# Layer 0's selective scan: delta turned by TensorE into PSUM instead of a transposed copy in memory

## The chip, the cores and the metric

The kernel runs on one core of one Trainium2 chip. The metric is the device time of one execution in microseconds (us), as the median of several runs of the whole program, four layers one after the other.

## The reference, cut to what matters

Layer 0 is a two-dimensional selective scan over 4 images of 64 x 64 tokens. Only the scan matters here:

```python
delta = jax.nn.softplus(delta + delta_bias[None, :, None])
def step(h, inp):
    u_i, d_i, b_i, c_i = inp
    dA = jnp.exp(d_i[..., None] * A)
    h = h * dA + (d_i * u_i)[..., None] * b_i[:, None, :]
    y = jnp.einsum('gdn,gn->gd', h, c_i)
    return (h, y)
```

There are 256 channels d with 16 states n each. Every image is scanned four times, with u read by rows, by columns, and both backwards, while delta, B and C are the same sequence in all four. The results are summed, normalised and projected. Layers 1 to 3 follow and are the same before and after the change.

## The kernel before, in words

**Chunks and passes.** A sequence of 4096 tokens is cut into 64 chunks of 64. The 256 channels are two halves h of 128. One step I of the loop treats one chunk of one half of one image, in all four directions; there are 4 x 2 x 64 = 512 steps. Sixty-four steps of one image and one half are called a pass. Direction is counted by j (0 forward, 1 backward) and kp (rows, columns). `quads` are groups of four chunks, whose deltas (`dp`, loaded by `load`, L564) and decays (`dA`, `decay`, L587) are kept together.

**One step** (L788 to L842). Its engines' work, in the order in which it is written out:

- `fetch(I + 2)` (L596) issues on SP the loads of the chunk two steps ahead: C broadcast (`ct`), u with tokens on the partitions (`xo`: 64 forward tokens, then 64 backward), delta with tokens on the partitions (`dt`: 64 tokens forward, then the same 64 backwards), and diagonals of B (`dg`).
- `diagonal(I + 1)` (L631) makes those diagonals on ACT in the passes of h = 0 and stores them for h = 1.
- `products(I, kp)` (L657): TensorE multiplies `du` (delta times u) with the diagonals of B, 16 small matmuls for each kp, into two tiles `db` of PSUM, one for each j. Each fp32 matmul appears as two records in the trace, so one call is 32 records. Three `db` tiles of two banks each exist in turn.
- `scan` (L678): DVE adds the carry to the first column of `db` (L684) and runs the scan (L687), once for each j. POOL then forms the carry for the next chunk (L694) and multiplies the states with C (L702).
- `total(I - 2, part)` (L709): TensorE sums the states over n into the PSUM tile `yp` (L722), in two parts of 16 records; after the second part ACT copies the four directions out (L736).
- `inputs(I + 1)` (L641): DVE forms `du` of the next step, `xo` times `dt` (L644).

So the order on TensorE is: products for kp 0, total's first part, side work, products for kp 1, side work, total's second part. On DVE: two scans, `inputs` of the next step, two scans. TensorE, ACT and DVE keep this written order (a manual schedule).

**Side work.** The generator `beside` is advanced by one piece (to its next `yield`) twice in a step, and a third time in every fourth step of h = 0. In passes of h = 0 it carries `back` of the previous image (normalisation and projection) and `front` of the next one; in passes of h = 1 it carries `middle` of the next image: the convolution (L376), transposes (L394), projections (L406, L424, L436) and the softplus that gives delta. What is left is run out at once shortly before the end of h = 1. For the first image, `front` and `middle` run ahead of the loop, outside the manual schedule.

**Where the transposed delta comes from.** At the end of each block of 512 tokens `middle` has delta, channels on the partitions, in `rs`. It stores it (`dl`). It then turns each half with four transposes (L465), copies the result out on ACT (L475), multiplies it with the matrix `flip` to reverse the tokens within each chunk (L470), and copies that out too. Both are stored to `dT` (L477), and `fetch` reads `dt` from there. That takes four pieces of `beside` per block, of 14.

**PSUM** [...]six in the three `db` tiles, one for `yp` (half used), and one (`bg`) for the side work.

Of the kernel before, what the change touches and what calls it, by code (L numbers as in the profile page):

```python
# [14 lines left out]
P = 128  # L15
B = 4
HW = 64
S = HW * HW
NT = S // P
D = 128  # L20
BLK = 512
# [6 lines left out]
TC = 64  # L28
NCHUNK = S // TC
NH0 = NST // 2  # L30
QC = 4
# [28 lines left out]
def tl(pool, shape, tag, dtype=F32, bufs=None):  # L60
    return pool.tile(shape, dtype, name=tag, tag=tag, bufs=bufs)
# [99 lines left out]
def layer0(cm, x, W, x1, also, kept):  # L161


    tc, nc = cm.tc, cm.nc
    wl = kept.enter_context(tc.tile_pool(name="l0k", bufs=1))
    dr = kept.enter_context(tc.tile_pool(name="l0dram", bufs=2, space=DRAM))
    with ExitStack() as ctx:
        ctx.enter_context(nc.allow_non_contiguous_dma(reason="parameters laid over partitions"))
        wp = ctx.enter_context(tc.tile_pool(name="l0w", bufs=1))
        big = ctx.enter_context(tc.tile_pool(name="l0big", bufs=3))  # L170
        tmp = ctx.enter_context(tc.tile_pool(name="l0t", bufs=10))
        t4 = ctx.enter_context(tc.tile_pool(name="l0t4", bufs=4))
        yb = ctx.enter_context(tc.tile_pool(name="l0y", bufs=2))
        p2 = ctx.enter_context(tc.tile_pool(name="l0p2", bufs=2))
        db = ctx.enter_context(tc.tile_pool(name="l0db", bufs=3, space=PSUM))
        pp = ctx.enter_context(tc.tile_pool(name="l0pp", bufs=1, space=PSUM))
# [30 lines left out]
            part = cm.ident[rows, rows]  # L207
            nc.vector.tensor_copy(mask[rows, :], part[:, ::-1] if r > 1 else part)

        flip = tl(wp, [P, P], "flip")  # L210
        nc.vector.memset(flip, 0.0)
        for p in range(2):
            half = slice(p * TC, (p + 1) * TC)
            nc.vector.tensor_copy(flip[half, half], cm.ident[half, half][:, ::-1])

        both = tl(wp, [P, TC], "both")
        nc.vector.tensor_copy(both[0:TC, :], cm.ident[0:TC, 0:TC])
        nc.vector.tensor_copy(both[TC:P, :], cm.ident[TC:P, TC:P])
# [17 lines left out]
        dA = []  # L236
        for i in range(2):
            t = tl(wp, [P, QC, 2, NH0, TC], f"dA{i}")
# [2 lines left out]
            dA.append(t)  # L241


        yp = tl(pp, [P, 2, 2, TC], "yp")

        BT = tl(wp, [P, NCHUNK, NST], "BT")

# [3 lines left out]
        for i in range(2):  # L251
            t = tl(wp, [P, 8, PADW], f"padded{i}")
# [9 lines left out]
        img = {}  # L262

        def begin(b):
            img[b] = {
                "zs": tl(dr, [P, 2, S], "zs"),
                "dl": tl(dr, [2, P, S], "dl_d"),
                "ct": tl(dr, [NCHUNK, NST, TC], "ct_d"),
                "xT": tl(dr, [2, S, P], "xT_d"),
                "dT": tl(dr, [2, NCHUNK, 2, TC, P], "dT_d"),  # L270
                "y0": tl(dr, [P, 2, S], "y0_d"),
                "yr": tl(dr, [P, 2, S], "yr_d"),
            }
# [91 lines left out]
        def middle(b, bank, pool, tag, ahead):  # L365

            ready = [shifted(i, pool, tag) for i in range(ahead)]
            for k in range(NBLK):
                cols = slice(k * BLK, (k + 1) * BLK)
                xa = []  # L370
                for h in range(2):
                    ps = bank()
                    x3 = ready.pop(0)
                    for dx in range(3):
                        for g in range(4):
                            nc.tensor.matmul(  # L376
                                ps[g * CG : (g + 1) * CG, :], lhsT=cdiag[:, 4 * h + g, dx, :],
                                rhs=x3[g // 2][:, g % 2, :].rearrange(
                                    "p (r w) -> p r w", w=PADW
                                )[:, :, dx : dx + HW],  # L380
                                start=(dx == 0), stop=(dx == 2),
# [10 lines left out]
                    ps = bank()  # L392
# [4 lines left out]
                    t = tl(tmp, [P, 4, P], "t2k")  # L397
# [5 lines left out]
                ps = bank()  # L403
# [16 lines left out]
                ps = bank()  # L420
                pb = ps[:, 0 : 8 * NST].rearrange("p (c n) -> p c n", n=NST)
                for c in range(8):
                    for j in range(2):
                        nc.tensor.matmul(  # L424
                            pb[j * TC : (j + 1) * TC, c, :],
                            lhsT=xr[0:n, c, :] if j else xd[0:n, c * TC : (c + 1) * TC],
                            rhs=cm.ident[0:n, RANK : RANK + NST], start=True, stop=True,
                        )
                nc.vector.tensor_copy(BT[:, 8 * k : 8 * k + 8, :], pb)
                rs = []  # L430
# [24 lines left out]
                    nc.sync.dma_start(img[b]["dl"][h, :, cols], r)  # L455
                    rs.append(r)

                yield
                for h in range(2):
                    t = None  # L460
                    for j in range(2):
                        ps = bank()
                        if j == 0:
                            for i in range(4):
                                nc.tensor.transpose(  # L465
                                    ps[:, i * P : (i + 1) * P], rs[h][:, i * P : (i + 1) * P],
                                    cm.ident,
                                )
                        else:
                            nc.tensor.matmul(  # L470
                                ps, lhsT=flip, rhs=t.rearrange("p t c -> p (t c)"),
                                start=True, stop=True,
                            )
                        t = tl(tmp, [P, 4, P], "t2k")
                        nc.scalar.copy(t, ps.rearrange("p (t c) -> p t c", c=P))  # L475
                        for i in range(2):
                            nc.sync.dma_start(  # L477
                                img[b]["dT"][h, 8 * k + i : 8 * k + 8 : 2, j]
                                .rearrange("t r c -> r t c"), t[i * TC : (i + 1) * TC],
                            )  # L480
                        yield

        def back(b, bank, tmp=tmp, t4=t4):

# [79 lines left out]
        def load(q):  # L564

            b, h, c = place(q * QC)
            cols = slice(c * TC, (c + QC) * TC)
            dp = tl(p2, [P, 2, QC, TC], "dp")
            for p in range(2):
                nc.sync.dma_start(  # L570
                    dp[p * TC : (p + 1) * TC].rearrange("p g c t -> p g (c t)"),
                    img[b]["dl"][h, :, cols].rearrange("(g d) t -> d g t", d=TC),
                )
            return {"dp": dp, "dA": dA[q % 2], "h": h}

        def begun(w):

# [18 lines left out]
        def fetch(I):  # L596

            b, h, c = place(I)
            ct = tl(p2, [P, NH0, TC], "ct", bufs=4)
            for p in range(2):  # L600
                nc.sync.dma_start(
                    ct[p * TC : (p + 1) * TC].rearrange("p n t -> p (n t)"),
                    img[b]["ct"][c, p * NH0 : (p + 1) * NH0, :].rearrange("n t -> (n t)")
                    .unsqueeze(0).to_broadcast([TC, NH0 * TC]),
                )
            xo = tl(p2, [P, 2, P], "xo", bufs=3)
            dt = tl(p2, [P, P], "dt", bufs=3)
            nc.sync.dma_start(dt, img[b]["dT"][h, c].rearrange("j r c -> (j r) c"))
            xT = img[b]["xT"][h]
            rows = (  # L610
                slice(c * TC, (c + 1) * TC), slice(c, S, TC),
                slice(S - (c + 1) * TC, S - c * TC), slice(TC - 1 - c, S, TC),
            )
            for j in range(2):
                for kp in range(2):
                    nc.sync.dma_start(
                        xo[j * TC : (j + 1) * TC, kp, :], xT[rows[2 * j + kp], :]
                    )
            dg = tl(p2, [P, NST, QR], "dg", bufs=3)
            if h:  # L620
                nc.sync.dma_start(dg, dg_d[c].rearrange("p (n t) -> p n t", t=QR))
            inp[I] = {"ct": ct, "xo": xo, "dg": dg, "dt": dt}

        def first(w):
            nc.scalar.activation(w["a0"], w["a0"], AF.Exp)
# [5 lines left out]
        def diagonal(q):  # L631

            if q["h"]:
                return
            for n in range(NST):
                nc.scalar.activation(  # L636
                    q["dg"][:, n, :], mask, AF.Copy, scale=BT[:, q["c"], n : n + 1]
                )
            nc.sync.dma_start(dg_d[q["c"]], q["dg"].rearrange("p n t -> p (n t)"))

        def inputs(q):  # L641

            q["du"] = tl(p2, [P, 2, P], "du")
            nc.vector.tensor_tensor(  # L644
                q["du"], q["xo"], q["dt"].unsqueeze(1).to_broadcast([P, 2, P]), ALU.mult
            )

        def after(later, earlier):
            tc.add_manual_dep(
                later.ins, earlier.ins.name,  # L650
                mybir.DependencyInfo(
                    mybir.DependencyClass.Sync, mybir.DependencyReason.DATA
                ),
                reason="row groups of one bank",
            )

        def products(q, kp):  # L657
            bs = [tl(db, [P, 2 * NH0, TC], "db") for _ in range(2)]
            mm = None
            for half in range(2):  # L660
                if half:
                    nc.tensor.drain()
                for i in range(8):
                    j, r, p = i // 4, i // 2 % 2, i % 2
                    g = r ^ half
                    rows = slice((2 * j + r) * QR, (2 * j + r + 1) * QR)
                    t0 = (r ^ j) * QR
                    nc.tensor.matmul(  # L668
                        bs[j][
                            p * TC : (p + 1) * TC, g * NH0 : (g + 1) * NH0, t0 : t0 + QR  # L670
                        ],
                        lhsT=q["du"][rows, kp, g * TC : (g + 1) * TC],
                        rhs=q["dg"][rows, p * NH0 : (p + 1) * NH0, :],
                        start=True, stop=True,
                    )
            return bs
# [97 lines left out]
        fetch(1)  # L774
        nxt = start(0)
        diagonal(nxt)
        inputs(nxt)
        beside, clock = None, [0]

# [7 lines left out]
        with tc.manual_schedule(engines=engines):  # L787
            for I in range(N):  # L788
# [27 lines left out]
                if I + 1 < N:  # L816
                    nxt = start(I + 1)
                    diagonal(nxt)
                bs = products(now, 0)
                scan(I, now, 0, bs, st, carry, new)  # L820
                if I > 1:
# [1535 lines left out]
```

## Time and profile before

| | |
|---|---|
| median of 3 runs | 10872.56 us (10855.62 to 10873.84) |
| profiled execution | 10860.27 us |
| its span | 10858.5 us |
| TensorE (PE) busy | 8928.9 us, 82% |
| VectorE (DVE) busy | 7823.8 us, 72% |
| ScalarE (ACT) busy | 5313.2 us, 49% |
| GpSimd (POOL) busy | 5452.4 us, 50% |
| before the loop of layer 0 | 0 to 341 us |
| the loop of 512 steps | 341 to about 6245 us |
| layers 1 to 3 | the rest |

A row of the profile reads: line, engine, operation, written tile <- read tiles with shapes, number of instructions | busy time in us, mean of one in ns | idle time of the engine just before them, and what ended most of it. PEld is TensorE's loading of weights, which overlaps its matmuls. The granted clock is the share of full speed that TensorE's throttle allowed. A row of the timeline gives the start and the duration in us, and in brackets the engine's idle time before it. Ends of matmuls are modelled, and spans on POOL are rough.

### The profile page before, as it was taken

Reading aid. Unit: us, or ns where it says so; the run is one execution under the profiler, and the core shown is the slowest. Engines: PE = TensorE matmul, PEld = TensorE weight load, DVE = VectorE, ACT = ScalarE, POOL = GpSimd, SP = SyncE. Lnnn points to the kernel's source line nnn. Section 1 sums busy time; section 2 is a strip of 40 time slices with the busy share of each in tenths; the row PEclk is TensorE's granted clock in tenths of the full one; section 3 lists DMA queues with packets and bytes.
Section 4 is the critical chain, followed back from the end, with each engine's and each line's share of the span. In section 5 each row is a group of like instructions: output and inputs, shape, how many; then the busy total and the mean of one; then the engine's idle time right before and its main releaser. Section 6 shows DMA issues by size and latency. Waiting matters only on the chain. (4 is left out here: it accounts for less than half of the span.)

```text
span 10858.5 us, 190052 instructions
## 1 busy us (share of the span) xinstructions
PE 8928.9 (82%) x72040; PEld 4226.5 (39%) x72040; DVE 7823.8 (72%) x10667; ACT 5313.2 (49%) x13151; POOL 5452.4 (50%) x2661
## 2 busy tenths in 40 slices
PE   6668998779887788887788846999999956998886
PEld 2333443334333333333333323444444434544442
DVE  1799999999999999999999965546361132445546
ACT  5557554556444565445532124767676613333321
POOL 0579999879888888888899920000000000000000
PEclk7789998889888889888888968999999976577767
DMA  5434554335443345443333231111100083012101
GB/s 150 105 91 128 145 140 110 103 98 153 131 119 110 109 117 141 130 119 102 99 94 94 74 117 38 36 35 36 32 27 16 16 226 70 26 37 57 41 20 47
DMA packets 1155618, 960.91 MB, mean 88 GB/s; under 512 B 191940, under 2 KB 905384, under 8 KB 1148312
## 3 DMA queue, kind: packets, MB, share of 16 engines
q1 hardware_dynamic: 1140888, 898.41, 29.2%
q0 software_dynamic: 13824, 50.34, 2.6%
q8 instruction: 579, 9.49, 0.4%
q14 instruction: 327, 2.68, 0.1%
HBM read 616.68 MB, written 331.61 MB: 87 GB/s over the span
## 5 line engine op out<-in xcount | busy, mean ns | idle before, releaser
L687 DVE TENSOR_TENSOR_SCAN big<-dA,db 128x1024 f32<-128x1024 f32 x2048 | 4679.5, 2286 | 81.9 <-PE db L668 3.1
L702 POOL TENSOR_TENSOR big<-big,ct 128x2048 f32<-128x2048 f32 x1024 | 4648.2, 4539 | 78.7 <-DVE big L687 0.2
L668 PE MATMUL db<-dg,du 32*64 32x256 f32 x32768 | 1952.0, 427 | 822.1 <-DVE db L684 674.5
L722 PE MATMUL yp<-big,both 128*64 128x256 f32 x16384 | 2368.9, 438 | 66.2 <-ACT yc L736 58.2
L722 PEld LDWEIGHTS yp<-big,both 128*64 128x64 f32 x16384 | 1250.6, 155 | 1152.0 <-issue 752.8
L668 PEld LDWEIGHTS db<-dg,du 32*64 32x64 f32 x32768 | 672.3, 138 | 2079.6 <-issue 1909.5
L736 ACT COPY yr<-yp 128x64 f32<-128x64 f32 x1024 | 224.4, 220 | 1618.2 <-PE yp L722 1617.8
L1480 PE MATMUL av<-e,x 128*128 128x512 f32 x2048 | 974.0, 592 | 4.6 <-ACT e L1475 4.6
L1431 PE MATMUL qk<-a,xT 128*128 128x512 f32 x2048 | 966.6, 594 | 8.7 <-ACT e L1435 7.9
L1435 ACT ACTIVATE e<-qk,nk 128x512 f32<-128x512 f32 x1024 | 693.3, 685 | 539.5 <-PE qk L1431 538.4
L591 ACT ACTIVATE dA<-dp,A 128x252 f32<-128x252 f32 x2048 | 866.1, 499 | 98.1 <-DVE big L687 48.3
L636 ACT ACTIVATE dg<-mask,BT 128x32 f32<-128x32 f32 x4096 | 898.5, 323 | 5.3 <-PE db L668 5.3
L1010 POOL TENSOR_TENSOR g_rs<-g_rs,qrow 128x4 f32<-128x4 f32 x32 | 41.1, 1285 | 1500.4 <-DVE g_rs L1009 1500.4
L694 POOL TENSOR_TENSOR cy<-big,a 128x32 f32<-128x32 f32 x1008 | 347.4, 345 | 571.3 <-DVE big L687 374.8
L1431 PEld LDWEIGHTS qk<-a,xT 128*128 128x128 f32 x2048 | 378.0, 190 | 462.4 <-issue 358.0
L1480 PEld LDWEIGHTS av<-e,x 128*128 128x128 f32 x2048 | 381.6, 190 | 434.8 <-issue 393.7
L1475 ACT ACTIVATE e<-e 128x1024 f32<-128x1024 f32 x510 | 538.8, 1056 | 15.5
L644 DVE TENSOR_TENSOR du<-xo,dt 128x256 f32<-128x256 f32 x512 | 533.1, 1041 | 12.8 <-DMA xo<-xT_d 12.8
L1956 ACT ACTIVATE e<-s 72x576 f32<-72x576 f32 x448 | 273.3, 643 | 512.2 <-PE s L1949 509.2
L1967 POOL COPY vp<-vt 72x160 f32<-72x160 f32 x56 | 19.6, 352 | 909.6 <-PE po L1973 906.8
L2189 DVE SCALAR_TENSOR_TENSOR tex<-x,gw,tex 128x128 f32<-128x128 f32 x768 | 264.2, 344 | 254.6 <-PE x L2183 239.8
L1913 DVE TENSOR_REDUCE mx<-s 96x6 f32<-96x864 f32 x224 | 226.0, 1047 | 291.0 <-PE s L1905 290.7
(528 smaller groups left out, 9883.4 us busy)
## 6 DMA issues: line engine op xcount, KB each, us to landing
ct<-ct_d SPq DMA_DIRECT2D x1024, 128.0 KB
xo<-xT_d SPq DMA_DIRECT2D x2048, 32.0 KB
dg_d<-dg SPq DMA_DIRECT2D x256, 256.0 KB
dg<-dg_d SPq DMA_DIRECT2D x256, 256.0 KB
t4k<-xc_d SPq DMA_DIRECT2D x384, 132.0 KB
dT_d<-t2k SPq DMA_DIRECT2D x256, 128.0 KB
dp<-dl_d SPq DMA_DIRECT2D x256, 128.0 KB
dt<-dT_d SPq DMA_DIRECT2D x512, 64.0 KB
```

The costliest lines, as they stand in the source:

```text
L591: nc.scalar.activation(w["dA"][:, :, g, n, 1:], w["dp"][:, g, :, 1:], AF.Exp, scale=A[:, w["h"], g, n : n + 1],)
L636: nc.scalar.activation(q["dg"][:, n, :], mask, AF.Copy, scale=BT[:, q["c"], n : n + 1])
L644: nc.vector.tensor_tensor(q["du"], q["xo"], q["dt"].unsqueeze(1).to_broadcast([P, 2, P]), ALU.mult)
L668: nc.tensor.matmul(bs[j][p * TC : (p + 1) * TC, g * NH0 : (g + 1) * NH0, t0 : t0 + QR], lhsT=q["du"][rows, kp, g * TC : (g + 1) * TC], rhs ...
L687: nc.vector.tensor_tensor_scan(st[:, u].rearrange("p n t -> p (n t)"), q["w"]["dA"][:, c % QC].rearrange("p g n t -> p (g n t)"), bs[j].re ...
L694: nc.gpsimd.tensor_tensor(new[:, us, :], st[:, us, :, TC - 1], quads[(I + 1) // QC]["a0"][:, (c + 1) % QC] .rearrange("p g n -> p (g n)"). ...
L702: nc.gpsimd.tensor_tensor(sv, sv, q["ct"].rearrange("p n t -> p (n t)").unsqueeze(1) .to_broadcast([P, 4, NH0 * TC]), ALU.mult,)
L722: nc.tensor.matmul(yp[p * TC : (p + 1) * TC], lhsT=both, rhs=st[:, :, p * NH0 + n, :], start=(n == 0), stop=(n == NH0 - 1),)
L1431: nc.tensor.matmul(ps, lhsT=me["xT"][:, kt * P : (kt + 1) * P], rhs=me["a"][k], start=True, stop=True,)
L1435: nc.scalar.activation(e[:, j, :], ps, AF.Exp, bias=me["nk"][:, kt : kt + 1], scale=2.0)
L1475: nc.scalar.activation(es[g + 2], es[g + 2], AF.Exp)
L1480: nc.tensor.matmul(avs[b, k], lhsT=img[b]["x"][:, kt, :], rhs=e[:, j, :], start=(kt == 0), stop=(kt == NT - 1),)
```

## The change

`middle` no longer makes a transposed copy of delta. It writes a second copy of delta, channels still on the partitions, with the tokens of each chunk in reverse (`rl`): one ACT copy and one store for each half, in two pieces of `beside` instead of four, and 11 pieces per block in all. `load` brings these reversed deltas (`dr`) for four chunks at a time, beside `dp`. `fetch` no longer loads `dt`.

A new function `deltas` turns the chunk's delta on TensorE: four matmuls with the identity, 64 channels by 64 tokens each, for j = 0 from `dp`, for j = 1 from `dr`. The results lie in PSUM, in the half of `yp`'s bank that was free; the tile is now called `yd`, `yp` is a view of its first half, and `dt` alternates between two quarters of the second. `deltas(I + 1)` stands ahead of `products(I, 0)` in the step. `inputs` is as it was, but reads `dt` from PSUM.

```diff
-        flip = tl(wp, [P, P], "flip")
...
-        yp = tl(pp, [P, 2, 2, TC], "yp")
+        yd = tl(pp, [P, BLK], "yd")
+        yp = yd[:, 0 : 4 * TC].rearrange("p (k j t) -> p k j t", k=2, j=2)
...
-                "dT": tl(dr, [2, NCHUNK, 2, TC, P], "dT_d"),
+                "rl": tl(dr, [2, P, S], "rl_d"),
...
-                yield
                 for h in range(2):
-                    t = None
-                    for j in range(2):
-                        ps = bank()
-                        if j == 0:
-                            for i in range(4):
-                                nc.tensor.transpose(
-                                    ps[:, i * P : (i + 1) * P], rs[h][:, i * P : (i + 1) * P],
-                                    cm.ident,
-                                )
-                        else:
-                            nc.tensor.matmul(
-                                ps, lhsT=flip, rhs=t.rearrange("p t c -> p (t c)"),
-                                start=True, stop=True,
-                            )
-                        t = tl(tmp, [P, 4, P], "t2k")
-                        nc.scalar.copy(t, ps.rearrange("p (t c) -> p t c", c=P))
-                        for i in range(2):
-                            nc.sync.dma_start(
-                                img[b]["dT"][h, 8 * k + i : 8 * k + 8 : 2, j]
-                                .rearrange("t r c -> r t c"), t[i * TC : (i + 1) * TC],
-                            )
-                        yield
+                    yield
+                    t = tl(tmp, [P, 8, TC], "t2k")
+                    nc.scalar.copy(
+                        t, rs[h].rearrange("p (c t) -> p c t", t=TC)[:, :, ::-1]
+                    )
+                    nc.sync.dma_start(
+                        img[b]["rl"][h, :, cols].rearrange("p (c t) -> p c t", t=TC), t
+                    )
...
-            return {"dp": dp, "dA": dA[q % 2], "h": h}
+            turned = tl(p2, [TC, 2, QC, TC], "dr")
+            nc.sync.dma_start(
+                turned.rearrange("p g c t -> p g (c t)"),
+                img[b]["rl"][h, :, cols].rearrange("(g d) t -> d g t", d=TC),
+            )
+            return {"dp": dp, "dr": turned, "dA": dA[q % 2], "h": h}
...
-            dt = tl(p2, [P, P], "dt", bufs=3)
-            nc.sync.dma_start(dt, img[b]["dT"][h, c].rearrange("j r c -> (j r) c"))
...
+        def deltas(I, q):
+            c = I % QC
+            q["dt"] = yd[:, 4 * TC + I % 2 * P : 4 * TC + (I % 2 + 1) * P]
+            for j in range(2):
+                src = q["w"]["dr"] if j else q["w"]["dp"]
+                for g in range(2):
+                    nc.tensor.matmul(
+                        q["dt"][j * TC : (j + 1) * TC, g * TC : (g + 1) * TC],
+                        lhsT=src[0:TC, g, c, :], rhs=cm.ident[0:TC, 0:TC],
+                        start=True, stop=True,
+                    )
...
                 if I + 1 < N:
                     nxt = start(I + 1)
                     diagonal(nxt)
+                    deltas(I + 1, nxt)
                 bs = products(now, 0)
```

The diff also removes the unused helper `after` and calls `deltas(0, nxt)` once ahead of the loop.

More of the change, by code (lines that the diff above doesn't have):

```diff
@@ L208, in layer0 @@
             nc.vector.tensor_copy(mask[rows, :], part[:, ::-1] if r > 1 else part)
-        flip = tl(wp, [P, P], "flip")
[L211 to L214, printed above, removed]
         both = tl(wp, [P, TC], "both")
@@ L621, in fetch @@
                 nc.sync.dma_start(dg, dg_d[c].rearrange("p (n t) -> p n t", t=QR))
-            inp[I] = {"ct": ct, "xo": xo, "dg": dg, "dt": dt}
+            inp[I] = {"ct": ct, "xo": xo, "dg": dg}
         def first(w):
@@ L646, in inputs @@
             )
[L648 to L655, printed above, removed]
         def products(q, kp):
             bs = [tl(db, [P, 2 * NH0, TC], "db") for _ in range(2)]
-            mm = None
             for half in range(2):
@@ L776, in layer0 @@
         diagonal(nxt)
+        deltas(0, nxt)
         inputs(nxt)
```

## The prediction

> **What bounds the kernel now.** I read the page first, for the engines' shares in the layer 0 slices, then the busy time by pass (image and half; 64 steps each), then the rows by shape, then one step in the timeline. The page's chain lists only lines of later stages, so this stage is argued from engines and waits.
>
> Busy time by pass (columns: PE, weight loads, DVE, ACT, POOL, granted clock, DMA):
> ```profile
> 1095.00:1785.00 690.00, 621.94 (x7014) 280.63 (x7012) 674.48 (x630) 337.09 (x800) 637.22 (x300) 0.93 0.50 134
> 1785.00:2573.00 788.00, 619.30 (x6454) 282.07 (x6452) 744.86 (x635) 447.78 (x1633) 672.17 (x314) 0.88 0.39 113
> 5592.00:6245.00 653.00, 529.01 (x6134) 241.70 (x6132) 642.67 (x571) 135.28 (x511) 636.00 (x294) 0.91 0.32 87
> ```
> DVE is busy 95 to 98% of each pass: it sets the pace. The passes from 341 to 6245 us hold the 512 steps, 11.53 us each on average; the last pass, which has no work beside the scans, takes 10.2. PE is next, with 1 to 3 us per step unused, then POOL. DMA is at half at most.
>
> The page's rows that matter, then the multiplication by itself (min/median/max):
> ```profile
> L687 DVE TENSOR_TENSOR_SCAN big<-dA,db 128x1024 f32<-128x1024 f32 x2048 | 4679.5, 2286 | 81.9 <-PE db L668 3.1
> L668 PE MATMUL db<-dg,du 32*64 32x256 f32 x32768 | 1952.0, 427 | 822.1 <-DVE db L684 674.5
> L722 PE MATMUL yp<-big,both 128*64 128x256 f32 x16384 | 2368.9, 438 | 66.2 <-ACT yc L736 58.2
> L644 DVE TENSOR_TENSOR du<-xo,dt 128x256 f32<-128x256 f32 x512 | 533.1, 1041 | 12.8 <-DMA xo<-xT_d 12.8
> ```
> ```profile
> L644 DVE TENSOR_TENSOR du<-xo,dt x512: 359/512/4772, 338.2 to 6230.5; 128x256 f32<-128x256 f32 x171
> ```
> PE waits for DVE (822 us), not the reverse. The multiplication's mean is twice its median, and its longest is one POOL product long (the big product takes 4.54 us): with both inputs in SBUF it sometimes stands until POOL's product is over.
>
> One step without side work, in the last pass:
> ```profile
> 5899.67 2.29 DVE L687 TENSOR_TENSOR_SCAN big<-dA,db 128x1024 f32<-128x1024 f32 x1
> ...
> 5901.09 3.27 PE L722 MATMUL yp<-big,both 128*64 128x256 f32 x16
> ...
> 5901.88 0.50 DVE L644 TENSOR_TENSOR du<-xo,dt 128x256 f32<-128x256 f32 x1
> ...
> 5904.29 2.11 PE L668 MATMUL db<-dg,du 32*64 32x256 f32 x32
> 5904.40 0.21 ACT L736 COPY yr<-yp 128x64 f32<-128x64 f32 x1 [7.55 <-PE yp L722]
> ...
> 5904.71 0.30 ACT L736 COPY yc<-yp 128x64 f32<-128x64 f32 x1
> ...
> 5907.12 0.16 DVE L684 TENSOR_TENSOR db<-db,cy 128x16 f32<-128x16 f32 x1
> ```
> Call the four scans of a step a, b, c, d. Scan b ends at 5901.96, du follows, then c and d, and scan a of the next step begins with its addition at 5907.12. Meanwhile PE does, in its own order, the second half of total (5901.09; it starts before du), then at once products for the next a and b, which end at 6.40, 0.7 us before DVE wants them. ACT's copies lie beside the products. The step is 10.04 us (next du at 5911.92).
>
> **The change part by part.**
>
> *du from PSUM.* The nearest rows are DVE products with one PSUM input, in the same passes:
> ```profile
> L513 DVE TENSOR_TENSOR t4k<-t4k,bg 128x512 f32<-128x512 f32 x50 | 31.6, 672 | 1.3 <-DMA t4k<-zs 1.0 <-PE bg L508 0.2
> ```
> 672 ns for 512 elements, close to its siblings L527 (683) and L454 (691), though POOL was as busy: no stall. Half the elements at some 1.04 ns each is 0.41 us. Bounds: 0.36 (the shortest du now) to 0.51 (its median). Saved on DVE: 533 - 512 x 0.41 = 323 us (272 to 349).
>
> *The turn (deltas).* Four matmuls of 64 rows, 64 columns, 64 moving, eight records. Low end by L424 (64 columns, 16 moving: 30 records in 1.10 us): 0.3 us. High end by L394 (four 128-wide transposes): 0.66. I take 0.5, nearer to transposes. Left out at the start of a step it would lie in PE's idle time; where it stands, ahead of the products of the same step, it is on the path below.
>
> *The new bank.* dt shares PSUM bank yd with yp. The Trainium skill, page "PSUM — Partial Sum Buffer", section "PSUM bank collisions raise a hardware error", says that two engines must not touch the same bank and partitions at once, whatever the columns, and that semaphores should guard by bank. So I expect waits by bank, not by address; no wait in this trace can show it, since yp was alone. By it three waits arise. du waits for total's first half: long done (it ends some 3 us before). The second half of total waits for du. The turn of the next step waits for ACT's four copies; behind it in PE's queue stand products and scan a of all that follows. A ring closes:
>
> scan b's end, du 0.41 + gap 0.04; release of PE 0.14 (scan's end 5909.60 to PE 5909.74); total's second half 2.31 (2368.9/1024); copies done 0.65 later (5904.36 to 5905.01); release 0.14; turn 0.5; products 1.95 (32 records took 1.94 to 2.11); release of DVE 0.1; additions and scans a and b 4.88 (5907.12 to 5912.00). Sum 11.12 us. DVE alone would need 10.04 - 0.09 = 9.95. The ring adds 1.17 x 512 = 599 us. Without the rule (waits by address) it adds nothing: that is the first rival.
>
> Total at full speed takes 1.95 us, and 3.27 in the step shown; its mean is 2.31. The skill's page "TensorE: Matmul & The Clock Gate", Part 1, ties the half clock to idle windows of some 3.4 us; by that the ring, whose gaps are 1 to 2 us, runs at 1.95 and makes 10.76, and the sum falls by 0.36 x 512 = 184. But the last pass was granted 0.91 with PE waits of under 1.5 us, so I take the trace's mean.
>
> *What the ring swallows.* DVE idles 1.17 us after scan d, so DVE's side work that is issued there (about 12 pieces in each h=0 pass, some of which are shorter, and 8 in each of three h=1 passes) loses up to that: 95 us. The 114 us that scans' additions wait for products today (by the line's waits) are the same wait and not paid twice: -114.
>
> *PE's side work.* PE's own step is 9.81 (two totals 2.31, two products 1.95, turn 0.5, wait for copies 0.79), so 1.31 us of side work fits. The middle stage has, per block, 2 x 2.78 + 2 x 0.66 + 1.9 + 1.1 + 2 x 1.44 (L436), some 12.5 us. Its yields fall from 14 to 11, so they lie in 5.5 steps: 2.27 a step, 0.95 too much, over 44 steps of three passes: +125. In the h=0 passes the mean is 1.6; I take 10 us each: +40. Bounds 0 to 250.
>
> *ACT late.* Total waits 58 us, 29 times, for copies that stand behind side work on ACT; products (1.95) used to cover part of that. Without the cover, 29 x 1.95 = +57 (0 to 150).
>
> *Removed from middle.* Transposes, flips and half the copies: off DVE, so nothing in the passes beyond the above. In the lead-in before 341 us, L454 ends at 233.65 and the next convolution starts at 236.69, 3.0 us behind the flips: 8 blocks x 3.0 = -24. The new copies are two per block of 0.59 on ACT (row of L475, 586 ns), never last.
>
> *DMA and queues.* SP loses 512 dt loads and 256 dT stores and gains 64 stores and 128 loads; it moves half the bytes. load now waits, on SP, for the turn of the fourth chunk; the fetch behind it waits for POOL's product of the step before anyway, which comes later: nothing. dr has four steps to land. Nothing here is last, so I count none of it.
>
> Sum: -323 + 599 - 95 - 114 + 165 + 57 - 24 = +265. The profiled execution took 10860.3 us (span 10858.5), 12 us under the median of the runs. 10860 + 265 = 11125, 2.4% above.
>
> **The rivals.**
>
> *Waits by address only.* Then du saves its 323, the lead-in 24, and PE pays 0.5 us in the crowded middle steps (132 x 0.5 = 66): 10,580. For: the slots are disjoint columns, and DVE is plainly the bound. Against: the bank rule. 0.14.
>
> *Ring at full clock.* Total 1.95, turn 0.3: ring 10.56, adding 0.61 x 512 = 312. Side work fitting is then 1.67, excess 0.6 x 132 = 79; swallowed 60: -323 + 312 - 60 - 114 + 79 + 57 - 24 = -73, 10,787, faster. The point from which the sign turns is a ring of about 10.65. For: most totals take 1.95. Against: the granted clock. 0.16.
>
> *More half clock.* PE now stands before total and before the turn; if half of all totals and products run at half speed, the ring is some 0.45 us longer, +230: 11,355. For: the clock falls where PE waits. 0.16.
>
> **How the numbers follow.** The ring as costed: 0.54, own range 10,950 to 11,290 (turn 0.3 to 0.66, side work 0 to 250, less what overlaps). 0.2% is about what a measurement of this kernel can tell from no change. Faster: 0.14 + 0.16 = 0.30; the ring's lower edge puts 0.05 within 0.2%; slower 0.65. The range leaves out the first rival and the far end of the third: 10,770 to 11,370.
>
> **What would show it.** du near 0.41 us with a maximum under 1 us; total's second half released by DVE du, and the turn by ACT's copies; PE idle before L668 for DVE gone, DVE idle before the additions for PE grown from 114 to several hundred us; the last pass near 11.1 us a step instead of 10.2; lead-in shorter by some 24 us. Wrong if total starts before du has ended, if the last pass gets shorter, or if du still shows 4 us.

## The result and the profile after

The changed kernel takes 10932.25 us (median of 5 runs, 10921.52 to 10954.61), the kernel before 10873.84 in the 5 runs beside it: a ratio of 1.0055, 95% interval 1.004 to 1.0071. The change makes the whole slower by half a per cent. The forecast was slower too, but by 2.4%. The profiled execution's span is 10938.0 us, 79.5 above that of before.

The rows of the page after the change; line numbers have moved (L672 is the scan, L653 products, L707 total, L669 the addition ahead of a scan, L630 the turn):

```profile
L672 DVE TENSOR_TENSOR_SCAN big<-dA,db 128x1024 f32<-128x1024 f32 x2048 | 4679.9, 2286 | 89.2 <-PE db L653 8.8
...
L707 PE MATMUL yd<-big,both 128*64 128x256 f32 x16384 | 2280.4, 426 | 406.6 <-DVE du L639 398.2
L653 PE MATMUL db<-dg,du 32*64 32x256 f32 x32768 | 1700.1, 424 | 304.2 <-DVE db L669 163.5
...
L669 DVE TENSOR_TENSOR db<-db,cy 128x16 f32<-128x16 f32 x2016 | 342.9, 170 | 531.2 <-PE db L653 502.7
L630 PE MATMUL yd<-ident,dp 64*64 64x64 f32 x2048 | 240.6, 241 | 551.0 <-ACT yc L721 534.6
```

The multiplication by itself, min/median/max in ns:

```profile
L639 DVE TENSOR_TENSOR du<-xo,yd x512: 360/395/422, 312.8 to 6312.1; 128x256 f32<-128x256 f32 x171
```

Two waits are new, both on PE: total waits for du (398 us), and the turn for ACT's copies (535 us). The old one, products waiting for DVE, has shrunk from 674 to 164, and the opposite has appeared: DVE's additions wait 503 us for products, where it was 114 (total us, times, longest; before, then after):

```profile
DVE db L684 <- PE db L668: 114.3, 127, 12.7
...
DVE db L669 <- PE db L653: 502.7, 297, 12.7
```

du has lost its stalls. Its longest is 422 ns where it was 4772, and all 512 take 203 us instead of 533.

Busy time by pass (columns: PE, weight loads, DVE, ACT, POOL, granted clock, DMA), for the same three passes as before:

```profile
1089.00:1875.00 786.00, 624.61 (x7428) 286.00 (x7426) 665.87 (x630) 325.90 (x780) 630.05 (x299) 0.88 0.39 110
1875.00:2625.00 750.00, 588.01 (x6965) 281.21 (x6963) 690.37 (x635) 448.00 (x1638) 663.79 (x315) 0.92 0.40 116
5674.00:6328.00 654.00, 500.15 (x6640) 239.15 (x6634) 628.09 (x571) 133.76 (x508) 624.81 (x295) 0.97 0.30 84
```

DVE was busy 98% of the first of these passes and is busy 85% of it now, so it no longer sets the pace there. Time of a step in us, from the starts of the scans (in the last pass, to the end of its last scan):

| pass | before | after | turn_later (below) |
|---|---|---|---|
| image 0, h=0 | 11.78 | 12.07 | 11.31 |
| image 0, h=1 | 10.78 | 12.28 | 11.10 |
| image 1, h=0 | 12.32 | 11.72 | 11.65 |
| image 1, h=1 | 11.53 | 12.37 | 11.17 |
| image 2, h=0 | 12.24 | 11.65 | 11.53 |
| image 2, h=1 | 11.59 | 12.20 | 11.08 |
| image 3, h=0 | 11.80 | 11.43 | 11.41 |
| image 3, h=1 (no side work) | 10.21 | 10.21 | 10.24 |

The 512 steps take 6010.8 us from first to last scan, 106.7 more than before; the lead-in ends 24.9 us earlier, and the rest differs by 2. DVE saved 330 us in du and lost 363 in idle time before scan a (101 before, 464 after; counted in the trace) and 32 before scan c. Of the remaining 42 us, 13 are three operations of a normalisation (L303, 0.22 us each before): each now took 4.6 us, as long as one product on POOL. Another 9 are the additions, which became a little longer; the rest was not followed.

A step without side work after the change, in the last pass:

```profile
5903.52 0.40 DVE L639 TENSOR_TENSOR du<-xo,yd 128x256 f32<-128x256 f32 x1
...
5903.97 1.95 PE L707 MATMUL yd<-big,both 128*64 128x256 f32 x16 [1.17 <-DVE du L639]
...
5906.28 0.30 ACT L721 COPY yc<-yd 128x64 f32<-128x64 f32 x1
...
5906.63 0.27 PE L630 MATMUL yd<-ident,dp 64*64 64x64 f32 x1 [0.71 <-ACT yc L721]
...
5907.02 0.69 PE L653 MATMUL db<-dg,du 32*64 32x256 f32 x16
...
5907.85 0.69 PE L653 MATMUL db<-dg,du 32*64 32x256 f32 x16 [0.15 <-issue]
...
5908.65 0.18 DVE L669 TENSOR_TENSOR db<-db,cy 128x16 f32<-128x16 f32 x1
...
5913.47 0.40 DVE L639 TENSOR_TENSOR du<-xo,yd 128x256 f32<-128x256 f32 x1
```

The predicted ring is there, link by link: du, total, copies, turn, products, the addition of scan a. But it takes 9.95 us from du to du, just what the prediction gave for DVE's own work: the addition at 5908.65 follows the products' end (5908.54) by 0.11 and starts, as the others do, a little before the scan ahead of it ends, with no wait.

And a step with side work, in image 1's h=1 pass. ACT has a softplus of the middle stage (L438 to L443) ahead of the copies:

```profile
3003.94 2.98 PE L707 MATMUL yd<-big,both 128*64 128x256 f32 x16
...
3005.86 0.69 ACT L441 ACTIVATE bg<-t2k,ones 128x512 f32<-128x512 f32 x1
3006.57 1.28 ACT L443 ACT_TABLE_LOAD   x1
3007.86 0.60 ACT L443 ACTIVATE t2k<-bg 128x512 f32<-128x512 f32 x1
...
3008.66 0.32 ACT L721 COPY yc<-yd 128x64 f32<-128x64 f32 x1
...
3009.02 0.36 PE L630 MATMUL yd<-ident,dp 64*64 64x64 f32 x1 [2.10 <-ACT yc L721]
...
3009.66 1.16 PE L653 MATMUL db<-dg,du 32*64 32x256 f32 x16
...
3012.22 0.18 DVE L669 TENSOR_TENSOR db<-db,cy 128x16 f32<-128x16 f32 x1 [4.25 <-PE db L653]
```

Total ends at 3006.92, but the copies are done only at 3008.98, after ACT's table load. The turn waits for them, the products stand behind the turn, and DVE idles 4.25 us. Not all of that is the copies. Against the step above they are 1.4 us later. Another 2.2 us come from total, turn and products, which run slower here (2.98, 0.64 and 2.46 us against 1.95, 0.39 and 1.52), and 0.7 from side work on PE, which holds up total. On the ring all of it adds up. The experiments ask which link makes the loss.

### The profile page after: what moved, and what is told of

The parts are those of the page before. It is cut to its first block, busy times and chain, and to the rows that moved or that the text cites. A ratio compares the mean times of both kernels' runs of the same rounds, so it can differ in the third digit from the quotient of the medians.

```text
span 10938.0 us, 196855 instructions
## 1 busy us (share of the span) xinstructions
PE 8738.2 (80%) x75752; PEld 4205.3 (38%) x75752; DVE 7531.3 (69%) x10664; ACT 5265.4 (48%) x13087; POOL 5378.8 (49%) x2661
## 5 line engine op out<-in xcount | busy, mean ns | idle before, releaser
L672 DVE TENSOR_TENSOR_SCAN big<-dA,db 128x1024 f32<-128x1024 f32 x2048 | 4679.9, 2286 | 89.2 <-PE db L653 8.8
L707 PE MATMUL yd<-big,both 128*64 128x256 f32 x16384 | 2280.4, 426 | 406.6 <-DVE du L639 398.2
L653 PE MATMUL db<-dg,du 32*64 32x256 f32 x32768 | 1700.1, 424 | 304.2 <-DVE db L669 163.5
L707 PEld LDWEIGHTS yd<-big,both 128*64 128x64 f32 x16384 | 1205.3, 152 | 1469.3 <-DVE du L639 575.1
L721 ACT COPY yr<-yd 128x64 f32<-128x64 f32 x1024 | 225.0, 220 | 1950.5 <-PE yd L707 1950.0
L653 PEld LDWEIGHTS db<-dg,du 32*64 32x64 f32 x32768 | 573.8, 136 | 1199.3 <-issue 1117.9
L669 DVE TENSOR_TENSOR db<-db,cy 128x16 f32<-128x16 f32 x2016 | 342.9, 170 | 531.2 <-PE db L653 502.7
L630 PE MATMUL yd<-ident,dp 64*64 64x64 f32 x2048 | 240.6, 241 | 551.0 <-ACT yc L721 534.6
L679 POOL TENSOR_TENSOR cy<-big,a 128x32 f32<-128x32 f32 x1008 | 298.2, 296 | 753.0 <-DVE big L672 690.6
L630 PEld LDWEIGHTS yd<-ident,dp 64*64 64x64 f32 x2048 | 167.2, 142 | 810.5 <-ACT yc L721 787.9
```

The lines of the kernel that those rows point to most:

```text
L630: nc.tensor.matmul(q["dt"][j * TC : (j + 1) * TC, g * TC : (g + 1) * TC], lhsT=src[0:TC, g, c, :], rhs=cm.ident[0:TC, 0:TC], start=True, s ...
L653: nc.tensor.matmul(bs[j][p * TC : (p + 1) * TC, g * NH0 : (g + 1) * NH0, t0 : t0 + QR], lhsT=q["du"][rows, kp, g * TC : (g + 1) * TC], rhs ...
L669: nc.vector.tensor_tensor(bs[j][:, :, 0], bs[j][:, :, 0], old[:, u, :], ALU.add)
L672: nc.vector.tensor_tensor_scan(st[:, u].rearrange("p n t -> p (n t)"), q["w"]["dA"][:, c % QC].rearrange("p g n t -> p (g n t)"), bs[j].re ...
L707: nc.tensor.matmul(yp[p * TC : (p + 1) * TC], lhsT=both, rhs=st[:, :, p * NH0 + n, :], start=(n == 0), stop=(n == NH0 - 1),)
```

## The experiments

The theory after the traces: the gain on DVE is real, and it is lost because the turn, which stands ahead of the products in PE's queue, waits for ACT's copies out of the same bank (theory A in the expectations). The rivals: total's wait for du (B), the side work pressed into fewer pieces (C), and the turn's own time on PE.

**turn_later.** Only the place of the turn changes.

```diff
-                    deltas(I + 1, nxt)
                 bs = products(now, 0)
+                if nxt:
+                    deltas(I + 1, nxt)
                 scan(I, now, 0, bs, st, carry, new)
```

> The changed kernel with the turn placed behind the products for kp 0 instead of ahead of them; nothing else differs. Theory A (the loss is the turn's wait for ACT's copies, which products and scan a stand behind): DVE's idle time before scan a falls from 464 us to about 150, and the time to about 10,620, faster than both kernels. Theory B (the loss is the second half of total waiting for du): the wait stays, idle before scan a stays above 350 us, time about 10,900. Theory C (the loss is the side work of the middle stage pressed into 11 pieces): about 10,900, with the h=1 passes still near 12.3 us a step.

Measured: 10651.07 us, ratio to before 0.9803 (0.9787 to 0.9818). Its longest waits on PE (total us, times, longest):

```profile
PE yd L707 <- DVE du L639: 396.1, 314, 6.6
PE db L653 <- DVE db L669: 239.3, 180, 13.5
PE yd L630 <- ACT yc L721: 46.6, 34, 6.1
```

The wait for the copies has gone from 535 to 47 us, since the products now run while ACT copies. Total's wait for du is as long as ever (396 us against 398). Idle time before scan a falls from 464 to 223 us, where about 150 was expected. This is theory A in the main, and neither B nor C. The same four matmuls, two lines further down, turn a loss of 0.55% into a gain of 2%.

**no_turn.** The turn is taken out of the loop; du reads the slot that was filled ahead of it.

```diff
-                    deltas(I + 1, nxt)
+                    nxt["dt"] = yd[:, 4 * TC : 4 * TC + P]
```

> The changed kernel without the turn in the loop: du is formed with the delta that was turned once ahead of the loop, so its values are those of the first chunk. du still reads the bank of yp and total's second half still waits for it. Theory A: no wait for ACT's copies is left ahead of the products, so about 10,600, no more than 30 us below the kernel with the turn placed later. Theory B: about 10,880. Theory C: about 10,880.

Measured: 10618.77 us, ratio 0.9771 (0.9755 to 0.9787). So in its later place the turn costs some 32 us in all (0.06 us a step), a sixth of the 0.39 us that it takes on PE. The granted clock differs too (0.853 of full speed without the turn, 0.867 with it), so this is the turn's price net of the clock. Total waits 413 us for du here too, with the time this low: that wait is not the loss.

**pace_14.** Three empty `yield`s are added per block of the middle stage.

```diff
                 for h in range(2):
                     yield
+                    if h:
+                        yield
                     t = tl(tmp, [P, 8, TC], "t2k")
...
+                yield
+                yield
```

> The changed kernel with three empty pieces of side work added to each block of the middle stage, so that a block has 14 pieces again as before the change. Theory A: within 40 us of the changed kernel's 10,932, since as many copies come late. Theory B: the same. Theory C: the h=1 passes of the first three images fall from 12.3 us a step to about 11.5, and the time to about 10,780.

Measured: 10930.44 us, ratio 1.0065 (1.0051 to 1.0079), against 10932.25 and 1.0055 of the changed kernel. The three h=1 passes stay at 12.2 to 12.4 us a step. Theory C is out: how densely the side work lies makes no difference that shows.

**old_path_psum_du.** The kernel before, with du reading a constant in the second half of yp's bank.

```diff
+        yd = tl(pp, [P, BLK], "yd")
+        yp = yd[:, 0 : 4 * TC].rearrange("p (k j t) -> p k j t", k=2, j=2)
...
+        nc.vector.tensor_copy(yd[:, 4 * TC : 4 * TC + P], nxt["dt"])
         inputs(nxt)
...
-                q["du"], q["xo"], q["dt"].unsqueeze(1).to_broadcast([P, 2, P]), ALU.mult
+                q["du"], q["xo"], yd[:, 4 * TC : 4 * TC + P].unsqueeze(1).to_broadcast([P, 2, P]), ALU.mult
```

> The kernel before with one change: du reads delta from a constant in the second half of yp's bank (the first chunk's delta, copied there once), while all transposes, stores and loads of the old path stay. So only POOL's hold on du goes and only total's wait for du comes. Theory A: du falls from 1.04 to 0.40 us, and the time by about 300 us, to 10,570. Theory B: total's wait gives it all back: 10,850 or more. Theory C makes the same of it as A.

Measured: 10649.28 us, ratio 0.9804 (0.9787 to 0.982). du takes 203 us, and the 512 steps 5694.9 instead of 5904.1. So of the 330 us that du no longer takes on DVE, 209 reach the end. The expectation of 300 took all of it; DVE's waits for products and POOL's carry, 136 us before and 235 here, take most of the difference. turn_later is as fast: its loop starts at 314 us instead of 351 here, which is about what its turn costs.

**copies_apart.** The copies read SBUF, so nothing on ACT touches the bank.

```diff
-                    yj = yp[:, kp, j, :]
+                    yj = cm.ident[:, 0:TC]
```

> The changed kernel, with the turn at its place ahead of the products, but ACT's four copies read a constant in SBUF in place of total's result (so the layer's output is not formed from the scan). Nothing on ACT touches the bank, so the turn waits for no copy; its PE time stays at the head of the step, and total still waits for du. Theory A (the wait for the copies is the loss): as with the turn placed later, 10,650 within 40 us. Theory P (it is the turn's PE time at the head of the step): near 10,900.

Measured: 10670.35 us, ratio 0.982 (0.9798 to 0.9842). With the turn at its old place at the head of the step, the loss is gone as soon as the copies leave the bank. It is the wait, not the place or the matmuls. This run frees more than the turn: the copies, which wait for nothing, now end some 5 us ahead of total, so ACT's other work is freed as well. With turn_later, which leaves the copies alone and comes to the same time, that is no rival.

**side_work_last.** The second piece of side work goes behind total and its copies.

```diff
-                if beside:
-                    next(beside, None)
                 if I > 1:
                     total(I - 2, 1)
+                if beside:
+                    next(beside, None)
```

> The changed kernel with the step's second piece of side work issued behind total's second part and its copies instead of ahead of them. Theory L (about half of the loss is copies that stand behind side work in ACT's queue: 94 steps with copies over 1 us late hold 244 of the 464 us of idle before scan a): fewer late steps, about 50, idle before scan a near 300 us, 10,790. Theory Q (PE's own load is the loss; the side work now stands between total and the turn): as much idle or more, 10,930 to 11,000.

Measured: 10840.38 us, ratio 0.9985 (0.9973 to 0.9998). Steps with copies done over 1 us after total's end fall from 94 to 55, and the idle time that follows them from 244 to 68 us. But the other steps' idle rises from 220 to 337, since side work on PE now stands in the ring itself: the time from the copies' end to the turn, 0.09 us in the mean of all steps, becomes 0.41. Both theories hold in part. By the ratios to the kernel before, about half of the expected gain came (0.7% of an expected 1.3%).

**turn_twice.** The turn is issued twice.

```diff
                     deltas(I + 1, nxt)
+                    deltas(I + 1, nxt)
```

> The changed kernel with the four matmuls of the turn issued twice, at the changed place; the second writes the same values. The turn takes 0.39 us of PE in a step without side work. Theory R (the ring from scan b over du, total, copies, turn and products to scan a is just full in steps without side work, as the trace of the changed kernel suggests: 9.95 us, as long as DVE's own work): the last pass grows by 0.39 x 64 = 25 us, and the whole by 100 to 200 us, to about 11,080. Theory S (the ring has slack there, and only late copies on ACT cost): the last pass stays at 10.2 us a step and the whole within 60 us of 10,932.

Measured: 11011.06 us, ratio 1.0149 (1.0125 to 1.0173). The changed kernel ran at another time, with the kernel before 13 us slower beside it: by the times the second turn costs 79 us, by the ratios 102. In the last pass the median step goes from 9.95 to 10.23 us, as theory R has it: the ring is full there and an addition shows. That is 0.28 us and not 0.39, since the second turn adds only 0.27 us on PE. The pass's mean hardly moves (10.21 to 10.22), because the changed kernel has some steps of 11.4 us in it, which are missing here; the last section shows them. So the 25 us that theory R gave this pass did not come, and the growth of the whole is at the lower end of its 100 to 200 us, or 21 us short of it, as one counts.

**du_between.** The turn later, total's first part ahead of scan a, du between scans a and b.

```diff
+                if I > 1:
+                    total(I - 2, 0)
-                scan(I, now, 0, bs, st, carry, new)
-                if I > 1:
-                    total(I - 2, 0)
+                scan(I, now, 0, bs, st, carry, new, nxt)
...
-                if nxt:
-                    inputs(nxt)
```

> The turn placed later, and besides total's first part issued ahead of scan a, and du formed between scans a and b instead of behind scan b. So du is done before total's second part is reached, and that wait of PE (396 us with the turn placed later) goes; du waits for total's first part instead, which ends about with scan a. Theory V (total's wait for du delays products for scan a in steps with side work): idle before scan a falls from 223 to about 100 us, 10,540. Theory W (that wait lies in time that PE has to spare): no gain, 10,640 to 10,700, with some new waits of du.

Measured: 10757.44 us, ratio 0.9911 (0.989 to 0.9932): slower than turn_later by 106, and outside what both theories gave. DVE's longest waits in it:

```profile
DVE du L639 <- PE yd L709: 172.4, 171, 5.3
DVE db L671 <- PE db L653: 121.6, 110, 12.7
DVE db L671 <- POOL cy L681: 63.6, 21, 10.3
```

PE's wait for du is gone, and DVE's additions wait less (122 us against 191). But du itself now waits 172 us for total's first part, on the engine that has nothing to spare. Theory V is out, and W is right that there is no gain, but not in its size. That the 396 us of PE lay mostly in time that PE had is shown better by turn_later and no_turn, which keep such a wait and are the fastest on this path.

## Why the prediction was right in its sign and wrong in its size

**du from PSUM:** right. 0.41 us was predicted, 0.395 is the median; 323 us were to be saved, 330 were.

**The waits by bank:** right, all of them. du never waits for total's first half, total waits for du (398 us), and the turn waits for the copies (535 us), though they touch other columns. The first rival, waits by address only, is out. But `yp` and `dt` are parts of one tile, `yd`, in one bank; whether the bank or the tile makes the order, no run can tell.

**The ring: wrong, and this is the step that failed.** Its links were right, its usual length was not, and the excess was charged to every step: 11.12 us and 1.17 x 512 = 599 us. Measured in a step without side work (the timeline above): du to total 0.45, total 1.95, copies 0.66, release 0.05, turn 0.39, products 1.52, release of DVE 0.11, additions and scans to the next du 4.82; 9.95 in all. A step whose links are at these sizes loses nothing. Of the 1.17 too much, 0.43 is products, 0.36 total, 0.23 the two releases of PE (with du), 0.11 the turn, 0.06 the additions and scans, less 0.02.

- *Products* had been taken from a call that was partly waiting for DVE (1.94 us); called late enough that nothing holds them, they take 1.52.
- *Total* had been taken at its mean over the layer, slow windows included, and the clock rule of the Trainium skill's page "TensorE: Matmul & The Clock Gate", Part 1, was set aside for it. The mean of total's second half did not change: 2.29 us before and after. But it is a mixture. After the change 110 of the 512 take over 2.5 us (124 before), and most others 1.95. In the last pass it is 12 of 63 (14 before), and they make the mean step 10.21 us, 0.26 above the 9.95; the forecast was 11.1.
- *The release of PE* was misread. It was counted from a scan's end, but PE's row names the addition ahead of the scan, which had ended at 5909.68, 0.06 us before PE began:

```profile
5909.52 0.16 DVE L684 TENSOR_TENSOR db<-db,cy 128x16 f32<-128x16 f32 x1
...
5909.74 1.45 PE L668 MATMUL db<-dg,du 32*64 32x256 f32 x24 [0.88 <-DVE db L684]
```

**What the ring costs** is what late and slow links add to it in some of the steps. Idle time before scan a rose by 363 us. Some 215 of it (29 before, 244 after) follow the steps whose copies end over 1 us after total (97 before, 94 after), and 148 (72 before, 220 after) the others. But not all of that 215 is the copies. In the 260 steps with idle time before scan a, set against the sizes above, the copies are too long by 185 us in sum, slow totals, turns and products by 248, and total's start is late by 184, mostly behind side work on PE. (Together that is more than the idle time, since DVE's own side work covers a part.) Slow totals and side work were there before. They show now because the wait for the copies and the turn, 0.66 + 0.05 + 0.39 us in every step, have used up the time that the ring had to spare. Moving the turn gives that time back, and so wins 241 of the 363 us and not the late copies alone.

The prediction had 57 us for late copies, because it charged each of the 29 waits the products' 1.95 us of lost cover, where the wait before had shown only what stuck out beyond that cover. The trace of before already had 97 such steps, with 210 us of lateness beyond the usual 0.66, and could have been read for them. For PE's side work it had 165, against the 148. So the sum was too high by 599 in one term and too low by 158 in another; what the ring was to swallow (-95 and -114) fell away with it. That the sign came out right is in part luck: with the ring at its usual length, and the two swallowed terms gone with it, the same sum gives -125 us, a gain.

**The pace:** the 11 pieces were counted on to crowd the middle stage (125 us of the 165); pace_14 shows no effect on the time.

**The lead-in:** 24 us predicted, 24.9 measured. That it fits to 1 us is luck: in the runs that share the changed lead-in the first scan starts at 309 to 317 us, and in old_path_psum_du, with the old one, at 351 instead of 341. **DMA and queues:** nothing predicted; du waited for a load once, 5.1 us (12.8 before).

**The rivals:** the second (a ring at full clock, 10,787) came nearer to the ring's length (10.56 us) but had the sign wrong, since it too left the late copies at 57 us. The third (more half clock) is not seen: there are no more slow totals than before, 110 against 124.

**Left open:** dt in a bank or a tile of its own was not tried, no run held the clock fixed, and some 20 us of smaller differences in the loop were not followed.

## What to carry to other kernels

Two uses of one PSUM tile and bank were ordered here as if they were one: the write to the free half waited for the reader of the other. If a bank must be shared, issue the write behind work that needs neither, so that the other reader's delay is covered; here that one move was worth 2.5% (ratios 1.0055 and 0.9803). When a new dependency closes a ring over several engines, give each link its usual size, its slow or late size, and how often each occurs. A mean charged to every step put the loss where it was not.

## What the runs showed of the hardware

More work on PE can come with a faster PE. In the last pass, where no side work runs, total's second part takes 1.95 us as a rule and 3.3 to 3.7 when it is slow. Of 63 such parts, all but one took over 2.5 us without the turn (no_turn, mostly 3.40), 30 with the turn later (turn_later), 12 with the turn at the changed place, and one with the turn issued twice, at the pass's very end. The pass's busy time in no_turn, turn_later and turn_twice, with the granted clock third from the end:

```profile
5348.00:6000.00 652.00, 542.91 (x6115) 250.18 (x6112) 629.07 (x569) 135.39 (x511) 624.17 (x294) 0.84 0.30 81
...
5387.00:6040.00 653.00, 545.83 (x6616) 256.61 (x6613) 626.48 (x571) 135.32 (x511) 623.89 (x294) 0.91 0.31 84
...
5768.00:6420.00 652.00, 498.52 (x7102) 246.35 (x7098) 629.50 (x571) 134.11 (x507) 624.53 (x294) 1.00 0.31 84
```

PE executes a thousand records more in turn_twice than in no_turn and is busy 44 us less. The time does not gain by it: the median step is 10.23 us in both, in no_turn because the slow total fills the ring, in turn_twice because the second turn does. The rule of the same page, Part 1, an idle window of some 3.4 us ahead of the half clock, does not account for this: PE's longest idle time in these steps is 1.17 us (total waits for du) in no_turn, in the changed kernel and in turn_twice alike. Nor does the amount of work alone: turn_later has as many records as the changed kernel and two and a half times its slow totals. What decides stays open; no run took one cause away alone. The changed kernel's last pass has 11 steps of 11 to 11.5 us and 12 slow totals: on a ring that has no slack, each such total shows in the step.
